# Scales loaded first, first features kept as halves, the last projection begun ahead of weight loads, the last norm by tiles: an attention and feed-forward block on one core

## The chip, the core and the metric

The kernel runs on one core of a Trainium2 chip. The core has a matrix engine (TensorE, PE), a vector engine (DVE), a scalar engine (ACT), GpSimd (POOL) and a queue engine (SP) that issues most of the transfers; ACT and POOL issue a few. The working memory is SBUF (128 partitions), matmul results go to PSUM[...], and inputs, outputs and scratch tensors lie in DRAM. The metric is the device time of one execution in microseconds.

## The reference

One token sequence of 4096 tokens with 256 features goes through attention with 16 heads and a feed-forward net, each between two layernorms and with a residual:

```python
x = x + _layernorm(attn(_layernorm(x)))
x = x + _layernorm(ffn(_layernorm(x)))
# attn: causal, 16 heads of 16 features
qkv = x @ w_attn + b_attn
logits = jnp.einsum('bhqd,bhkd->bhqk', q, k) * scale        # causal mask
out = softmax(logits) @ v;  return out @ w_proj + b_proj
# ffn: weights are -1, 0 or 1, each output feature has a scale
_tlin = lambda x, w, s: jnp.einsum('bsi,oi->bso', x, w) * s
h = silu(_tlin(x, w1_w, w1_s)) * _tlin(x, w2_w, w2_s)       # 256 -> 1024
h = gelu(_tlin(h, h1_w, h1_s))                               # 1024 -> 1024
h = gelu(_tlin(h, h2_w, h2_s))
return _tlin(h, w3_w, w3_s)                                  # 1024 -> 256
```

All inputs and the output are float32.

## The kernel before

The tokens are cut into eight blocks of 512 (`QB`, `NB` = 8), each of four tiles of 128 tokens (`NT`). The program has two stages. From `manual_schedule` on, the order of the instructions on every engine is the order in which the Python program issues them; only the few instructions ahead of it are placed by a scheduler.

**Attention.** `prep(j)` normalizes block j of x, transposes it into `xT` (ACT copy, L460), and makes queries, keys and values. The main loop goes over 32 items (j, g): a block of queries and a group of four heads. For each it makes products of queries and keys twice: once for the row maxima (`MaxUnit`, reduced on DVE), and once for the exponentials (`ScoreUnit`, ACT); on the diagonal POOL masks the exponentials (L611). `Values` multiplies them with the values and with a column of ones, so that each head's row sums come out beside the weighted values. The result of an item is copied by ACT to `av_sb` (L650) and stored by SP to a DRAM scratch (`avd`, L652).

**Background work.** `Background` holds a queue of generators. Each `yield True` ends a step; the loop calls `step()` or `pace()` between its own instructions, and a step issues what lies up to the next yield. `prep` runs there, and `project(j)`: it loads x again and the row sums (L187, L191), after three steps takes their reciprocals on DVE (L194), stores these to DRAM (L196), loads the weighted values and, spread over partitions, the reciprocals (L200, L201), multiplies them on POOL (L208), multiplies with the projection's weights (TensorE, L218), takes the layernorm, adds x and stores the block (`x1`, L240). `norm_block(j)` loads such a block, normalizes it and transposes it (L260) to features on partitions; its callback `done` receives the two PSUM banks. During the last items of attention it is run for block 0, with `first_features` as the callback (ACT copies to `xT0`, L718). Projections of blocks 0 to 6 run in attention, that of block 7 in the feed-forward.

**Weights.** `halve_weights` rounds the ternary weights to the float32r type and tests whether they fit it exactly; `flag` says so, and a branch (`values_load`, L1006, L1007) takes `feed_forward(True)` where they do. The profiled run took it.

**Feed-forward.** Every activation is kept as two float32r halves, high and low part, and each product is made once for either. The loop goes over the eight blocks: `w1` and `w2` (eight feature chunks, `za`, `zb`), Silu on ACT, product on DVE (`fa`, L961), `settle` on DVE into the halves `ha` (L910, L911); two layers `h1`, `h2` (eight chunks each, Gelu on ACT, L974, `settle`); and `w3` by tiles of tokens (`pyf`, L987), scaled by `s3` on DVE (L994). After the fourth tile the block's layernorm follows (L996 to L999) and one store (L1000). After every chunk there is one `bg.step()`, in the two layers of block 0 two. At the start, `keep_features(0)` splits `xT0` into halves (ACT L925, DVE L927), SP issues sixteen loads of the `h2` weights (L174) and one of `w3` (L885), and only then, from the first steps, what `project(7)` loads. Four scale vectors and the broadcast `s3` are loaded by POOL's queue between the stages (L837, L846).

Buffers: in attention `o` and `inv` hold a projection's inputs, `T` the transposed block; in the feed-forward `activations(2, ..)` takes tiles of a pool with two buffers.

Of the kernel before, what the change touches and what calls it, by code (L numbers as in the profile page):

```python
# [10 lines left out]
F32 = mybir.dt.float32  # L11
F32R = mybir.dt.float32r
AF = mybir.ActivationFunctionType
ALU = mybir.AluOpType
# [3 lines left out]
P = 128  # L18
QB = 512
# [48 lines left out]
def sandwich_kernel(  # L68
# [70 lines left out]
        nc.vector.bn_aggr(mv[:, t, :], st)  # L139

    def layernorm_rstd(mv):
        ve = stat.tile([P, NT], F32, tag="ve", name="ve")
        nc.vector.tensor_scalar_add(ve, mv[:, :, 1], EPS)  # L143
        rstd = stat.tile([P, NT], F32, tag="rstd", name="rstd")
        nc.gpsimd.tensor_tensor(rstd, ve, neghalf, ALU.pow)  # L145
        return rstd

    def normalize(dst, src, mv, rstd, t, engine=nc.vector):
        engine.tensor_scalar(  # L149
            dst, src, mv[:, t, 0:1], rstd[:, t : t + 1], ALU.subtract, ALU.mult  # L150
        )
# [119 lines left out]
        mybir.EngineType.SP,  # L271
    }


    xT0 = const.tile([P, DC, QB], F32, tag="xT0", name="xT0")


    with ExitStack() as actx:
# [16 lines left out]
        class Room:  # L295
# [3 lines left out]
                return two_banks(name)[:, 0, :]  # L299

            def features(self, j):
                return [wk1.tile([P, DC, QB], F32, tag=t, name=f"{t}_{j}") for t in ("o", "inv")]

            def tokens(self, j):
                return wk1.tile([P, NT, D], F32, tag="y", name=f"y_{j}")
# [409 lines left out]

        def first_features(pts):
            for c in range(DC):
                nc.scalar.copy(xT0[:, c, :], pts[c])  # L718

        items = [(j, g) for j in range(NB) for g in range(G)]  # L720
        count = [NT * (j + 1) for j, g in items]
# [110 lines left out]
        bg.finish()  # L832


    def load_scale(pool, src, tag):
        s = pool.tile([P, FC], F32, tag=tag, name=tag)
        nc.gpsimd.dma_start(out=s, in_=src.rearrange("(c p) -> p c", p=P))  # L837
        return s

    fs = ctx.enter_context(tc.tile_pool(name="fs", bufs=1))  # L840
    s1 = load_scale(fs, w1_s, "s1")
    s2 = load_scale(fs, w2_s, "s2")
    sh1 = load_scale(fs, h1_s, "sh1")
    sh2 = load_scale(fs, h2_s, "sh2")
    s3 = fs.tile([P, D], F32, tag="s3", name="s3")
    nc.gpsimd.dma_start(out=s3, in_=w3_s.partition_broadcast(P))  # L846

    def feed_forward(halves):


# [4 lines left out]
        with ExitStack() as fctx:  # L855
# [23 lines left out]

            w3_r = fw.tile([P, FC, D], F32R, tag="w3", name=f"w3_{parts}")  # L880
            w3_sb = w3_r.bitcast(F32)
            if halves:
                tiles = {**W, "h2": weight_pieces("h2", TAGS["h2"])}
                load_pieces(rounded["h2"], tiles["h2"])
# [14 lines left out]
            def activations(n, name):  # L899

                return [
                    hp.tile([P, n, QB], F32, tag=f"h{n}{p}", name=f"{name}{p}")
                    for p in "hl"[:parts]
                ]

# [15 lines left out]
            def keep_features(j):  # L921
                def done(pts):
                    xT = xTs[j] = activations(DC, f"xTf{parts}_{j}")
                    for c in range(DC):
                        nc.scalar.copy(single(xT[0][:, c, :]), pts[c])  # L925
                        if halves:
                            nc.vector.tensor_tensor(  # L927
                                single(xT[1][:, c, :]),
                                pts[c],
                                single(xT[0][:, c, :]),  # L930
                                ALU.subtract,
                            )
                return done
# [12 lines left out]
                        )  # L946
                return ps

            room, bg = Room(), Background()
            keep_features(0)([xT0[:, c, :] for c in range(DC)])  # L950
            bg.add("project", project(NB - 1, room), PROJECT)
            for j in range(NB):
                xT = xTs[j]
                ha = activations(FC, f"ha{parts}_{j}")
                for oc in range(FC):
                    za = linear("w1", oc, xT, DC, f"za{parts}_{j}_{oc}")
                    zb = linear("w2", oc, xT, DC, f"zb{parts}_{j}_{oc}")
                    sl = f2.tile([P, QB], F32, tag="sl", name=f"sl{parts}_{j}_{oc}")
                    nc.scalar.activation(sl, za, AF.Silu, scale=s1[:, oc : oc + 1])  # L959
                    h = chunk(ha, oc, f"fa{parts}_{j}_{oc}")  # L960
                    nc.vector.scalar_tensor_tensor(  # L961
                        h, zb, s2[:, oc : oc + 1], sl, ALU.mult, ALU.mult
                    )
                    settle(ha, oc, h)
                    bg.step()
                if j + 1 < NB:
                    bg.add("norm", norm_block(j + 1, room, keep_features(j + 1)), NORM)
                src = ha
                for layer, (key, sc) in enumerate((("h1", sh1), ("h2", sh2))):
                    hb = activations(FC, f"hb{parts}_{j}_{layer}")  # L970
                    for oc in range(FC):
                        z = linear(key, oc, src, FC, f"z{parts}_{j}_{layer}_{oc}")
                        h = chunk(hb, oc, f"fb{parts}_{j}_{layer}_{oc}")
                        nc.scalar.activation(h, z, AF.Gelu, scale=sc[:, oc : oc + 1])  # L974
                        settle(hb, oc, h)
                        bg.step()
                        if j == 0:
                            bg.step()
                    src = hb
                bg.finish()  # L980
                y = f1.tile([P, NT, D], F32, tag="yf", name=f"yf{parts}_{j}")
                mv = stat.tile([P, NT, 2], F32, tag="mv", name=f"mvo{parts}_{j}")
                for t in range(NT):
                    ps = ps_f.tile([P, QB], F32, tag="f", name=f"pyf{parts}_{j}_{t}")
                    for c in range(FC):
                        for i, part in enumerate(src):
                            nc.tensor.matmul(  # L987
                                ps[:, 0:D],
                                lhsT=single(part[:, c, t * P : (t + 1) * P]),
                                rhs=(w3_r if halves else w3_sb)[:, c, :],  # L990
                                start=(c == 0 and i == 0),
                                stop=(c == FC - 1 and i == parts - 1),
                            )
                    nc.vector.tensor_tensor(y[:, t, :], ps[:, 0:D], s3, ALU.mult)  # L994
                    layernorm_stats(y[:, t, :], mv, t)
                rstd = layernorm_rstd(mv)  # L996
                for t in range(NT):
                    normalize(y[:, t, :], y[:, t, :], mv, rstd, t)
                    nc.gpsimd.tensor_tensor(y[:, t, :], y[:, t, :], xb[j][:, t, :], ALU.add)  # L999
                nc.sync.dma_start(  # L1000
                    out=out[j * QB : (j + 1) * QB, :].rearrange("(t p) d -> p t d", p=P),
                    in_=y,
                )


    low = nc.values_load(flag, min_val=0, max_val=1)  # L1006
# [38 lines left out]
```

## Time and profile before

| | us |
|---|---|
| median of 3 runs | 2574.32 (2571.3 to 2575.26) |
| the profiled execution | 2574.63 |
| its span, first to last instruction | 2572.9 |
| TensorE busy | 2439.2 |
| DVE busy | 1824.1 |
| ACT busy | 1257.2 |
| POOL busy | 575.2 |
| first score matmul (L508) | 61.73 |
| last attention product (L641) starts | 1852.89 |
| first feed-forward matmul (L940) starts | 1857.38 |
| last store issued (L1000) | 2567.23 |

Times in the trace's answers count from the first instruction. In a timeline each row is a start, a duration, the engine (PE is a matmul, PEld the load of its weights, SPq the issue of a transfer), the source line, the operation, and `out<-in` with the shapes; in brackets stands how long the engine was idle before it and what released it. The page cuts the span into 40 slices of 64.3 us and gives the busy share of each in tenths.

### The profile page before, as it was taken

The numbers are of one execution on the slowest core, as the hardware profiler recorded it, in microseconds if no ns is written. First come the engines' busy times: TensorE is split into PE (matmuls) and PEld (weight loads), VectorE is DVE, ScalarE is ACT, GpSimd is POOL, SyncE is SP. The second block draws the span as 40 slices with busy tenths as digits, with TensorE's granted clock in tenths as the row PEclk, the third lists the DMA queues.
The fourth block names the chain that finished last, engine by engine and source line by source line (L and its number), as shares of the span: only waits on it lengthen the run. The fifth ranks groups of instructions, "written<-read, shape, count | busy, mean of one in ns | idle before, by whom it ended". The sixth has DMA issues, their size and how long they took to land. (4 is left out here: it accounts for less than half of the span.)

```text
span 2572.9 us, 40118 instructions
## 1 busy us (share of the span) xinstructions
PE 2439.2 (95%) x15237; PEld 1444.8 (56%) x15237; DVE 1824.1 (71%) x3965; ACT 1257.2 (49%) x1490; POOL 575.2 (22%) x869
## 2 busy tenths in 40 slices
PE   5899999999999999999999999999989999999998
PEld 2454445445445544554455554544468877887786
DVE  2687788879788987898899898986055445544553
ACT  1335466556566655666577666766712222222221
POOL 2325333332242234322322222000120000000000
PEclk8779899899999999999999999999999999999999
DMA  4444244232233323324212232111120000000000
GB/s 156 144 152 154 88 135 153 99 129 74 91 108 123 120 83 130 109 79 141 66 62 95 83 96 72 57 45 55 42 90 17 17 1 17 17 17 1 17 9 10
DMA packets 134777, 202.73 MB, mean 79 GB/s; under 512 B 14864, under 2 KB 59536, under 8 KB 134576
## 3 DMA queue, kind: packets, MB, share of 16 engines
q1 hardware_dynamic: 132624, 198.75, 23.3%
q8 instruction: 122, 2.00, 0.3%
q10 hardware_dynamic: 1776, 1.18, 0.2%
q0 software_dynamic: 176, 0.15, 0.1%
q14 instruction: 79, 0.65, 0.1%
HBM read 137.91 MB, written 62.13 MB: 78 GB/s over the span
## 5 line engine op out<-in xcount | busy, mean ns | idle before, releaser
L606 ACT ACTIVATE e<-s 128x1024 f32<-128x1024 f32 (+3 forms) x1175 | 1040.6, 936 | 618.5 <-PE s L591 611.5
L521 DVE TENSOR_REDUCE mx<-pm 128x1 f32<-128x512 f32 x1792 | 1112.4, 682 | 160.4 <-PE pm L508 145.8
L508 PE MATMUL pm<-k,q 64*128 64x512 f32 (+3 forms) x2304 | 636.8, 460 | 56.8 <-DVE mx L521 40.7
L508 PEld LDWEIGHTS pm<-k,q 64*128 64x128 f32 x2304 | 326.5, 190 | 567.3 <-DVE mx L521 394.7
L641 PE MATMUL av<-e,v 128*32 128x512 f32 (+3 forms) x4608 | 591.1, 584 | 2.9 <-POOL e L611 2.9
L591 PE MATMUL s<-q,k 64*128 64x512 f32 (+3 forms) x2304 | 476.3, 395 | 7.6 <-DVE y L226 3.1
L591 PE MATMUL s<-mrow,ones 64*128 64x512 f32 (+3 forms) x2304 | 461.6, 384 | 0.0
L525 DVE CUSTOM_DVE_ANT_0 pm<-pm,mask 128x384 f32<-128x384 f32 (+3 forms) x512 | 239.8, 517 | 75.3 <-PE pm L508 71.4
L974 ACT ACTIVATE fb<-z,sh 128x512 f32<-128x512 f32 x128 | 88.1, 688 | 396.6 <-PE z L940 377.8
L591 PEld LDWEIGHTS s<-q,k 64*128 64x128 f32 x2304 | 237.0, 191 | 79.0 <-issue 19.3
L591 PEld LDWEIGHTS s<-mrow,ones 64*128 64x128 f32 x2304 | 241.8, 191 | 38.6 <-DVE mrow L565 0.7
L611 POOL TENSOR_SCALAR_AFFINE_SELECT e<-e 128x256 f32<-128x256 f32 x256 | 102.2, 407 | 647.6 <-ACT e L606 645.9
L145 POOL TENSOR_TENSOR rstd<-ve,neghalf 128x4 f32<-128x4 f32 x32 | 32.9, 1027 | 847.7 <-DVE ve L143 822.1
L940 PE MATMUL z<-hb_0h,h 128*128 128x512 f32 x512 | 203.7, 398 | 0.0
L940 PE MATMUL z<-hb_0l,h 128*128 128x512 f32 x512 | 202.2, 395 | 0.0
L641 PEld LDWEIGHTS av<-e,v 128*32 128x32 f32 x4608 | 92.6, 109 | 148.8 <-issue 130.0
L910 DVE CAST hb_1h<-fb 128x512 fp32r<-128x512 f32 x64 | 27.4, 428 | 149.9 <-ACT fb L974 149.9
L910 DVE CAST hb_0h<-fb 128x512 fp32r<-128x512 f32 x64 | 27.5, 430 | 139.4 <-ACT fb L974 139.4
L940 PEld LDWEIGHTS z<-hb_0h,h 128*128 128x128 f32 x512 | 96.8, 189 | 22.9
L940 PEld LDWEIGHTS z<-hb_0l,h 128*128 128x128 f32 x512 | 96.8, 189 | 22.1
L959 ACT ACTIVATE sl<-za,s 128x512 f32<-128x512 f32 x64 | 44.1, 689 | 131.4 <-DVE fa L961 66.4
L693 POOL CAST wh<-wc 128x256 fp32r<-128x256 f32 x88 | 34.9, 397 | 261.8 <-DMA wc<-in_h_t_dram 197.1
(235 smaller groups left out, 2430.9 us busy)
## 6 DMA issues: line engine op xcount, KB each, us to landing
k<-k SPq DMA_DIRECT2D x288, 256.0 KB
q<-q SPq DMA_DIRECT2D x64, 256.0 KB
x<-in_x_dram SPq DMA_DIRECT2D x16, 512.0 KB
k<-hik SPq DMA_DIRECT2D x32, 256.0 KB
k<-lok SPq DMA_DIRECT2D x32, 256.0 KB
q<-hiq SPq DMA_DIRECT2D x32, 256.0 KB
q<-loq SPq DMA_DIRECT2D x32, 256.0 KB
avd<-av_sb SPq DMA_DIRECT2D x32, 256.0 KB
```

The source lines that it names most:

```text
L508: nc.tensor.matmul(ps[:, 0:n], lhsT=qT[j, g][pr][r, t * P : (t + 1) * P], rhs=kT[G * j + g, c, pr][r, 0:n], start=True, stop=True,)
L521: nc.vector.tensor_reduce(self.mx[:, h, c : c + 1], ps[:, 0:n], AX.X, ALU.max)
L525: nc.vector.tensor_tensor_reduce(out=ps[:, 0:n], in0=ps[:, 0:n], in1=mask[:, QB - n : QB], scale=1.0, scalar=-3.0e38, op0=ALU.add, op1=ALU ...
L591: nc.tensor.matmul(self.ps[i][:, self.q0 :], lhsT=(self.k, ones[pr])[m][r, :], rhs=(qT[j, g][pr], mT[j, g])[m][r, self.q0 :], start=(m == ...
L606: nc.scalar.activation(e[:, at : at + n, q0:], ps[:, :, q0:], AF.Exp)
L611: nc.gpsimd.affine_select(out=at, in_=at, compare_op=ALU.is_ge, fill=0.0, base=0, pattern=[[0, 2], [1, P]], channel_multiplier=-1,)
L641: nc.tensor.matmul(self.av[h * HW : (h + 1) * HW, q0:], lhsT=vb[kt // NT][:, kt % NT, o : o + HW], rhs=es[h // 2][:, h % 2, q0:], start=(k ...
L693: nc.gpsimd.tensor_copy(hi, w)
L910: nc.vector.tensor_copy(hi, full)
L940: nc.tensor.matmul(ps, lhsT=w[c], rhs=single(part[:, c, :]), start=(c == 0 and i == 0), stop=(c == kc - 1 and i == parts - 1),)
L959: nc.scalar.activation(sl, za, AF.Silu, scale=s1[:, oc : oc + 1])
L974: nc.scalar.activation(h, z, AF.Gelu, scale=sc[:, oc : oc + 1])
```

## The change

Five things are edited. (1) The four scales and `s3` are loaded at the program's start, still on POOL's queue, into the pool of constants. (2) `first_features` writes block 0's features as two halves during attention: ACT copies the high part, DVE subtracts it from the PSUM bank for the low part. The feed-forward uses them directly, so that `keep_features(0)` goes. To make room, the projection in attention shares the buffer `T` with `prep` in place of a buffer `inv`, and the feature tiles of the feed-forward move to a pool with one buffer. (3) `project(7)` is created and advanced to its first yield ahead of the loads of `h2` and `w3`, so its loads of x and of the row sums come before them in SP's queue; the later steps of the projection each come one step earlier. (4) The layernorm at the end of a block is a function `leave`; for the last block it runs for every tile of tokens one tile behind, with an rstd and a store for each. (5) The last addition of the last tile is on DVE, the others stay on POOL.

```diff
--- before.py
+++ after.py
@@ -139,10 +139,11 @@
         nc.vector.bn_aggr(mv[:, t, :], st)
 
     def layernorm_rstd(mv):
-        ve = stat.tile([P, NT], F32, tag="ve", name="ve")
+        n = mv.shape[1]
+        ve = stat.tile([P, n], F32, tag=f"ve{n}", name="ve")
         nc.vector.tensor_scalar_add(ve, mv[:, :, 1], EPS)
-        rstd = stat.tile([P, NT], F32, tag="rstd", name="rstd")
-        nc.gpsimd.tensor_tensor(rstd, ve, neghalf, ALU.pow)
+        rstd = stat.tile([P, n], F32, tag=f"rstd{n}", name="rstd")
+        nc.gpsimd.tensor_tensor(rstd, ve, neghalf[:, 0:n], ALU.pow)
         return rstd
 
     def normalize(dst, src, mv, rstd, t, engine=nc.vector):
@@ -271,8 +272,22 @@
         mybir.EngineType.SP,
     }
 
-
-    xT0 = const.tile([P, DC, QB], F32, tag="xT0", name="xT0")
+    def load_scale(pool, src, tag):
+        s = pool.tile([P, FC], F32, tag=tag, name=tag)
+        nc.gpsimd.dma_start(out=s, in_=src.rearrange("(c p) -> p c", p=P))
+        return s
+
+    s1 = load_scale(const, w1_s, "s1")
+    s2 = load_scale(const, w2_s, "s2")
+    sh1 = load_scale(const, h1_s, "sh1")
+    sh2 = load_scale(const, h2_s, "sh2")
+    s3 = const.tile([P, D], F32, tag="s3", name="s3")
+    nc.gpsimd.dma_start(out=s3, in_=w3_s.partition_broadcast(P))
+
+
+    xT0 = [
+        const.tile([P, DC, QB], F32R, tag=f"xT0{p}", name=f"xT0{p}") for p in "hl"
+    ]
 
 
     with ExitStack() as actx:
@@ -299,7 +314,7 @@
                 return two_banks(name)[:, 0, :]
 
             def features(self, j):
-                return [wk1.tile([P, DC, QB], F32, tag=t, name=f"{t}_{j}") for t in ("o", "inv")]
+                return [wk1.tile([P, DC, QB], F32, tag=t, name=f"{t}o_{j}") for t in ("o", "T")]
 
             def tokens(self, j):
                 return wk1.tile([P, NT, D], F32, tag="y", name=f"y_{j}")
@@ -715,7 +730,9 @@
 
         def first_features(pts):
             for c in range(DC):
-                nc.scalar.copy(xT0[:, c, :], pts[c])
+                hi, lo = (t[:, c, :] for t in xT0)
+                nc.scalar.copy(hi, pts[c])
+                nc.vector.tensor_tensor(lo, pts[c], hi, ALU.subtract)
 
         items = [(j, g) for j in range(NB) for g in range(G)]
         count = [NT * (j + 1) for j, g in items]
@@ -832,19 +849,6 @@
         bg.finish()
 
 
-    def load_scale(pool, src, tag):
-        s = pool.tile([P, FC], F32, tag=tag, name=tag)
-        nc.gpsimd.dma_start(out=s, in_=src.rearrange("(c p) -> p c", p=P))
-        return s
-
-    fs = ctx.enter_context(tc.tile_pool(name="fs", bufs=1))
-    s1 = load_scale(fs, w1_s, "s1")
-    s2 = load_scale(fs, w2_s, "s2")
-    sh1 = load_scale(fs, h1_s, "sh1")
-    sh2 = load_scale(fs, h2_s, "sh2")
-    s3 = fs.tile([P, D], F32, tag="s3", name="s3")
-    nc.gpsimd.dma_start(out=s3, in_=w3_s.partition_broadcast(P))
-
     def feed_forward(halves):
 
 
@@ -879,6 +883,9 @@
 
             w3_r = fw.tile([P, FC, D], F32R, tag="w3", name=f"w3_{parts}")
             w3_sb = w3_r.bitcast(F32)
+            room, bg = Room(), Background()
+            last_projection = project(NB - 1, room)
+            next(last_projection)
             if halves:
                 tiles = {**W, "h2": weight_pieces("h2", TAGS["h2"])}
                 load_pieces(rounded["h2"], tiles["h2"])
@@ -899,7 +906,9 @@
             def activations(n, name):
 
                 return [
-                    hp.tile([P, n, QB], F32, tag=f"h{n}{p}", name=f"{name}{p}")
+                    (f1 if halves and n == DC else hp).tile(
+                        [P, n, QB], F32, tag=f"h{n}{p}", name=f"{name}{p}"
+                    )
                     for p in "hl"[:parts]
                 ]
 
@@ -946,9 +955,30 @@
                         )
                 return ps
 
-            room, bg = Room(), Background()
-            keep_features(0)([xT0[:, c, :] for c in range(DC)])
-            bg.add("project", project(NB - 1, room), PROJECT)
+            xTs[0] = [t.bitcast(F32) for t in xT0]
+            if not halves:
+                xTs[0] = activations(DC, "xTf0")
+                nc.vector.tensor_tensor(xTs[0][0], *xT0, ALU.add)
+            bg.add("project", last_projection, PROJECT)
+            due = []
+
+            def leave(j, y, mv, ts, rstd):
+
+                for i, t in enumerate(range(ts.start, ts.stop)):
+                    nc.vector.tensor_scalar(
+                        y[:, t, :], y[:, t, :], mv[:, t, 0:1], rstd[:, i : i + 1],
+                        ALU.subtract, ALU.mult,
+                    )
+                    (nc.vector if (j, t) == (NB - 1, NT - 1) else nc.gpsimd).tensor_tensor(
+                        y[:, t, :], y[:, t, :], xb[j][:, t, :], ALU.add
+                    )
+                nc.sync.dma_start(
+                    out=out[j * QB + ts.start * P : j * QB + ts.stop * P, :].rearrange(
+                        "(t p) d -> p t d", p=P
+                    ),
+                    in_=y[:, ts, :],
+                )
+
             for j in range(NB):
                 xT = xTs[j]
                 ha = activations(FC, f"ha{parts}_{j}")
@@ -993,14 +1023,14 @@
                             )
                     nc.vector.tensor_tensor(y[:, t, :], ps[:, 0:D], s3, ALU.mult)
                     layernorm_stats(y[:, t, :], mv, t)
-                rstd = layernorm_rstd(mv)
-                for t in range(NT):
-                    normalize(y[:, t, :], y[:, t, :], mv, rstd, t)
-                    nc.gpsimd.tensor_tensor(y[:, t, :], y[:, t, :], xb[j][:, t, :], ALU.add)
-                nc.sync.dma_start(
-                    out=out[j * QB : (j + 1) * QB, :].rearrange("(t p) d -> p t d", p=P),
-                    in_=y,
-                )
+                    if j == NB - 1:
+
+                        one = slice(t, t + 1)
+                        due.append((j, y, mv, one, layernorm_rstd(mv[:, one, :])))
+                        while len(due) > (t < NT - 1):
+                            leave(*due.pop(0))
+                if j < NB - 1:
+                    leave(j, y, mv, slice(0, NT), layernorm_rstd(mv))
 
 
     low = nc.values_load(flag, min_val=0, max_val=1)
```

## The prediction

> **What bounds the kernel now.** First the page: TensorE is busy in 95% of the span, so an edit counts only where TensorE stands still or a serial stretch lies open. The slices tell where: full from the third slice on except around slice 29, at the change of stage.
>
> ```profile
> PE 2439.2 (95%) x15237; PEld 1444.8 (56%) x15237; DVE 1824.1 (71%) x3965; ACT 1257.2 (49%) x1490; POOL 575.2 (22%) x869
> PE   5899999999999999999999999999989999999998
> PEclk8779899899999999999999999999999999999999
> ```
>
> Then the timeline of single engines where the diff works. At the change of stage, POOL's and TensorE's rows (start, duration, then in brackets the idle time and its releaser):
>
> ```profile
> 1850.65 0.41 POOL L611 TENSOR_SCALAR_AFFINE_SELECT e<-e 128x256 f32<-128x256 f32 x1 [0.39 <-ACT e L606]
> 1851.26 1.14 POOL L837 DMA_DIRECT2D s<-in_w_s_dram  x1 [0.20 <-issue]
> 1852.42 0.42 POOL L611 TENSOR_SCALAR_AFFINE_SELECT e<-e 128x256 f32<-128x256 f32 x1
> ...
> 1852.89 0.41 PE L641 MATMUL av<-e,v 128*32 128x128 f32 x4 [1.36 <-POOL e L611]
> 1857.38 0.80 PE L940 MATMUL za<-xTf_0h,w 128*128 128x512 f32 x1 [4.08 <-ACT xTf_0h L925]
> ```
>
> A scale's load sits in POOL's queue between the last two masks, so TensorE waits 1.36 us; then 4.08 us for the copy of the first features (L925), whose target is free only when the last attention store has landed. Further on, DVE, TensorE and the end:
>
> ```profile
> 1876.94 0.55 DVE L194 RECIPROCAL sums<-sums 128x64 f32<-128x64 f32 x1 [7.63 <-DMA sums<-avd]
> 1878.12 0.51 PE L940 MATMUL z<-ha_0h,h 128*128 128x512 f32 x1 [3.42 <-DVE fa L961]
> 1926.01 2.21 PE L260 MATMUL ptf<-ident,yn 128*128 128x128 f32 x8 [3.75 <-DVE yn L149]
> 2562.70 1.02 POOL L145 TENSOR_TENSOR rstd<-ve,neghalf 128x4 f32<-128x4 f32 x1 [79.86 <-DVE ve L143]
> 2563.75 2.19 DVE L149 TENSOR_SCALAR yf<-yf,mvo,rstd 128x256 f32<-128x256 f32 x4 [1.13 <-POOL rstd L145]
> 2564.24 2.96 POOL L999 TENSOR_TENSOR yf<-yf,x 128x256 f32<-128x256 f32 x4 [0.53 <-DVE yf L149]
> 2567.23 0.38 SPq L1000 DMA_DIRECT2D out_dram<-yf  x1
> ```
>
> DVE stands 7.63 us before block 7's reciprocal because its input was asked for at 1869.12, behind 5 MB of weights. The last block's norm is one serial chain after the last matmul. The start is serial too, and DVE and TensorE wait there for loads:
>
> ```profile
> 9.09 0.17 DVE L320 TENSOR_SCALAR bqk<-bqk 128x2 f32<-128x2 f32 x1 [9.09 <-DMA bqk<-in_b_attn_dram]
> 9.49 2.04 PE L756 MATMUL pb<-wp,bv 128*128 128x256 f32 x4 [9.49 <-DMA wp<-in_w_proj_dram]
> ```
>
> [...] the mean clock is 0.51 in 1855-1862 and 0.79 in 1878-1886 and in 1926-1934 (3.4 us of 8 at half), each beside a stall of 3.4 to 4.1 us, with matmuls 0.43 us apart instead of 0.23. So a stall that goes takes some 1.5 us more with it, and a new one of that length brings it back. [...] the sums, issued last on SP's queue, landed last; and while the scale loads ran (1857 to 1861) the core moved 312, 210, 130 and 145 GB/s against some 365 after.
>
> **The change part by part.** The sum is against the profiled execution (2574.63 us, span 2572.9), 0.3 us above the median of 2574.32.
>
> *Scales first, at the start: a loss.* The five POOL loads now begin at about 1 us; they issue in 1.14+0.91+1.75+0.57 = 4.4 us. POOL has that: after its memsets it waits from 3.5 to 14.4, and ident, now 1.1 us later, is first read at 9.17. But the DMA engines have not: their share is 0.94, 1.08 and 1.17 in the three windows from 2 to 8 us, and bqk and wp land at the end of that. Bounds: the loads' own 0.14 MB at 380 GB/s is 0.4 us; from the rates above, four microseconds at 200 instead of 365 lose 1.9 us in the worst stretch, and with the earlier scale loads some 3.5. Everything up to the first scores hangs on this chain, so I take +2.0, range +0.3 to +3.5.
>
> *Halves of the first features.* In attention, two subtractions from PSUM are added on DVE (L927's kind, 0.69 us each). They also hold both score buffers longer: TensorE's next scores waited for the second copy until 1719.67, and would wait for the second subtraction until about 1720.5. +0.8; from 0 (DVE has 2.3 us free soon after) to +1.7.
>
> *The change of stage.* With POOL's queue clear, the last mask starts at 1851.1 and the last products at 1851.55 instead of 1852.89: -1.34. Nothing is copied, so the first feed-forward matmul has only the branch (0.5 us of flag load) before it: about 1852.4 instead of 1857.38. What is late next is ACT: in the new order the Silu table load (1.28) itself waits for za, so Silu ends at 1853.5+1.28+0.69 and the first fa runs at 1855.55 instead of 1861.57. From there DVE sets the pace, 1.86 us for each of eight features, as in later blocks. 6.0 us earlier.
>
> *Projection begun ahead.* The load of x and of the sums are the first things SP issues after the last attention store; the sums wait for that store to land (2.7 us after its issue in the trace, so 1855.4), and the sixteen h2 loads behind them start at 1856, 1.4 us later than now. They are not needed until the second layer, 50 us on. The reciprocal stands one feature earlier and finds its sums there: the 7.63 us go. First-layer product 0 ended at about 1885.2; now it ends at 1855.55+15.3+0.5+0.35 = 1871.7: 13.5 us earlier.
>
> Then comes a new wait. The reciprocals' store and the two row-sum loads come after h2 and w3 in SP's order. 5 MB at 362 KB/us from 1857 are through at 1871.1, so the store lands at about 1872.3. In the trace POOL's first product began 5.16 us after the store's landing, its second 7.48; without one 256 KB load, which now goes ahead (1.4 us at 180 KB/us), that is 1876.0 and 1878.4, and the second ends at 1879.7. The new order puts half of the projection after product 1 (3.72 us), at 1875.4, where formerly both halves came after product 2. TensorE therefore stands 4.4 us, and with the half clock loses 1.7 more. Product 3 starts at 1879.75+1.8+3.7+1.8+1.7 = 1888.8 instead of 1895.88. So of the 13.5 us stay 7.1. If the inverse came in time 13.2 would stay; if it came 4 us later still, 3.5.
>
> *The shifted steps.* As every step is one earlier, the variance of block 7's tokens is issued right after product 3's start, not behind its settling, and block 1's normalization stands before the settling of second-layer feature 1. Relative to product 3 it started at 29.57 us (1925.45); now: product 0 of the second layer ends at 22.3, Gelu 0.7, settling 1.1, statistics 0.8, rstd 1.2, hence 26.15. The transposes wait some 0.6 us instead of 3.75[...]: -3.4 and -1.2. Block 1's load comes at 17.4 after product 3's start, before DVE has settled feature 6 at 16.8 plus its own work, so it adds at most 0.6 on DVE, whose result is needed later. -4.6, range -2 to -5.
>
> *The last norm by tiles.* Only tile 3 remains after the last matmul: up to ve unchanged (2562.6), rstd 1.0, normalize 0.4, add on DVE 0.45, with POOL's add of tile 2 (0.8) beside it; the two stores go one after the other at 2564.55 and 2565.0, against 2567.23. The last store is 128 KB instead of 512, which took 1.7 us in packets: -1.2. More small instructions on DVE and POOL beside the matmuls (POOL 1.0+0.8 of 1.92 us for a tile) may delay tile 3 by 0.3. -3.2, range -2 to -4.5.
>
> *At nothing.* The inverse shares the buffer of xT: projections and preparations follow each other in one queue, and the nearest pair in the trace (last use of xT at 130, load of the inverse at 166.6) has 36 us between. Single feature buffers in the feed-forward: the first layer has read them before the next norm writes. If either cover were gone it would show as new idle time of ACT before L460 or before the xTf copies.
>
> Sum: +2.0+0.8-7.1-4.6-3.2 = -12.1. From the median: 2562.2 us.
>
> **Rivals.** (1) The inverse comes in time, because the weights drain faster than 362 KB/us now that no scale loads are between: -18.3, 2556. For it: 370-390 in undisturbed microseconds; against: that is 1 us, and 4.4 are missing. (2) The inverse is 3 us later than I say or the start loses its full price: -7 to -9, 2566. For it: SP's issues took up to 1.49 us each with a deep queue. (3) Slower: the shifted start changes the clock of the first 330 us. The slices show it at 0.7 to 0.9 there, and a half-clock window of 3.4 us costs 1.7. It decides only from ten additional windows (17 us against 12.1): about 2580. [...] (4) The gains vanish: the first feed-forward matmul still waits, since its bank or ACT's table holds it, and the new wait eats the rest: 2572.
>
> **How the numbers follow.** Main case 0.50; (1) 0.20; (2) 0.17; (3) 0.07; (4) 0.06. The predicted time is the main case's, 2562.2. Bounds of its parts reach from -18 to -5; the range 2555.5 to 2570 leaves out cases (3), (4) and the edges of (1) and (2). A measurement of this kernel tells about 0.2%, 5.1 us, from no change, so faster means below 2569.2: the main case, (1), and most of (2), 0.83; same 0.10; slower 0.07.
>
> **What would show it.** Right: bqk and wp landing at 11 to 12 us; the first scores' stage shifted by as much; no wait of the last products on a mask over 0.3 us; first L949 matmul (za) under 1 us after the last product; no wait of DVE before the reciprocal; a wait of py for POOL of 3 to 6 us followed by half clock; transposes of block 1 waiting under 1 us; the last store 4 us after the last matmul. Wrong: a za that waits 3 us or more, a py without a wait, or a first score at an unchanged time.

## The result, and the profile after

| | before | changed |
|---|---|---|
| median, us | 2575.3 (2571.3 to 2576.84, 6 runs) | 2557.97 (2555.09 to 2564.41, 6 runs) |
| ratio to before | | 0.9939, 95% interval 0.9924 to 0.9953 |
| profiled execution, us | 2574.63 | 2558.75 |
| its span, us | 2572.9 | 2557.0 |

The change makes the kernel 0.6% faster, 17 us where 12 were forecast. First the page of the changed kernel: the busy time of the engines, the slices of TensorE and its clock.

```profile
PE 2424.5 (95%) x15237; PEld 1442.7 (56%) x15237; DVE 1822.2 (71%) x3969; ACT 1256.1 (49%) x1488; POOL 575.1 (22%) x871
...
PE   4899999999999999999999999999989999999998
...
PEclk8789999899999999999999999999999999999999
```

TensorE's busy time fell by 14.7 us (2439.2 to 2424.5) with the same 15237 matmuls. Idle time that goes does not lower busy time, so something else must have happened too: the matmuls themselves take less time. The slices do not show it, because it is spread thin.

The timeline at the start, then at the change of stage:

```profile
11.92 0.17 DVE L335 TENSOR_SCALAR bqk<-bqk 128x2 f32<-128x2 f32 x1 [11.92 <-DMA bqk<-in_b_attn_dram]
12.61 2.05 PE L773 MATMUL pb<-wp,bv 128*128 128x256 f32 x4 [12.61 <-DMA wp<-in_w_proj_dram]
...
1852.64 0.77 PE L656 MATMUL av<-e,v 128*32 128x128 f32 x8 [0.17 <-POOL e L626]
1853.46 0.58 ACT L665 COPY av_sb<-av 128x512 f32<-128x512 f32 x1 [1.13 <-PE av L656]
1854.10 0.50 PE L949 MATMUL za<-xT0h,w 128*128 128x512 f32 x1 [0.69 <-ACT av_sb L665]
1855.37 1.28 ACT L989 ACT_TABLE_LOAD   x1 [1.32 <-PE za L949]
1857.38 0.75 DVE L991 SCALAR_TENSOR_TENSOR fa<-zb,s,sl 128x512 f32<-128x512 f32 x1 [71.92 <-ACT sl L989]
1863.19 0.55 DVE L195 RECIPROCAL sums<-sums 128x64 f32<-128x64 f32 x1
1883.01 1.22 PE L219 MATMUL py<-wp,oi_2h 128*128 128x256 f32 x2 [5.90 <-POOL oi_2h L209]
1886.53 2.93 PE L219 MATMUL py<-wp,oi_2h 128*128 128x256 f32 x6 [2.30 <-POOL oi_2h L209]
1921.74 1.64 PE L261 MATMUL ptf<-ident,yn 128*128 128x128 f32 x8 [0.88 <-DVE yn L150]
```

wp lands 3.1 us later than before (12.61, not 9.49). The wait for the last mask is 0.17 us instead of 1.36, that of the first feed-forward matmul 0.69 instead of 4.08, and the reciprocal has no bracket: it no longer waits. The projection's matmuls (py) have a new wait of 5.90 + 2.30 us. Block 1's transposes (ptf) wait 0.88 instead of 3.75. At the end of the program (the rows are the last tile's, except the four stores, of which the first is for tile 0):

```profile
2548.01 4.75 SPq L975 DMA_DIRECT2D out_dram<-yf  x4
...
2550.52 0.58 POOL L146 TENSOR_TENSOR rstd<-ve,neghalf 128x1 f32<-128x1 f32 x1 [0.64 <-DVE ve L144]
...
2551.13 0.81 DVE L968 TENSOR_SCALAR yf<-yf,mvo,rstd 128x256 f32<-128x256 f32 x1 [0.44 <-POOL rstd L146]
2551.98 0.43 DVE L972 TENSOR_TENSOR yf<-yf,x 128x256 f32<-128x256 f32 x1
```

To see where the time comes from, take the same instruction in both traces and subtract its starts; the offset's change from one milestone to the next is what that stretch gained or lost. As in the prediction, the first layer is `h1` and the second `h2`, and a product is one feature chunk of 16 matmuls, whose end the Gelu on ACT marks. (The recorded expectations below count `w1`/`w2` as the first layer, so `h1` and `h2` are the second and third there.) Three of the milestones, first in the kernel before:

```profile
1885.39 0.69 ACT L974 ACTIVATE fb<-z,sh 128x512 f32<-128x512 f32 x1 [3.39 <-PE z L940]
...
1900.04 0.69 ACT L974 ACTIVATE fb<-z,sh 128x512 f32<-128x512 f32 x1 [6.48 <-PE z L940]
...
2561.30 0.42 DVE L994 TENSOR_TENSOR yf<-pyf,s 128x256 f32<-128x256 f32 x1 [0.81 <-PE pyf L987]
```

and then in the changed one:

```profile
1873.50 0.69 ACT L1004 ACTIVATE fb<-z,sh 128x512 f32<-128x512 f32 x1 [3.11 <-PE z L949]
...
1899.19 0.69 ACT L1004 ACTIVATE fb<-z,sh 128x512 f32<-128x512 f32 x1 [4.68 <-PE z L949]
...
2549.08 0.42 DVE L1024 TENSOR_TENSOR yf<-pyf,s 128x256 f32<-128x256 f32 x1 [0.30 <-PE pyf L1017]
```

| up to | offset, us | this stretch |
|---|---|---|
| last but one attention item (copy of `av_sb`) | +1.5 | +1.5 |
| Gelu of the first layer's product 0 | -11.9 | -13.4 |
| Gelu of its product 3 | -0.85 | +11.0 |
| last Gelu before block 1's transposes | -1.4 | -0.55 |
| next Gelu, after the transposes | -5.8 | -4.4 |
| last `yf` scaling (L1024) | -12.2 | -6.4 |
| end of span | -15.9 | -3.7 |

The fourth and sixth rows are the surprise: almost nothing of the diff runs there, and yet 7 us come from them, in steps of 0.09 us per product of 16 matmuls.

### The profile page after: what moved, and what is told of

Same layout as the page of the kernel before. It is cut to its first block, busy times and chain, and to the rows that moved or that the text cites. A ratio compares the mean times of both kernels' runs of the same rounds, so it can differ in the third digit from the quotient of the medians.

```text
span 2557.0 us, 40127 instructions
## 1 busy us (share of the span) xinstructions
PE 2424.5 (95%) x15237; PEld 1442.7 (56%) x15237; DVE 1822.2 (71%) x3969; ACT 1256.1 (49%) x1488; POOL 575.1 (22%) x871
## 5 line engine op out<-in xcount | busy, mean ns | idle before, releaser
L146 POOL TENSOR_TENSOR rstd<-ve,neghalf 128x4 f32<-128x4 f32 (+1 forms) x35 | 34.3, 979 | 829.7 <-DVE ve L144 803.7
L991 DVE SCALAR_TENSOR_TENSOR fa<-zb,s,sl 128x512 f32<-128x512 f32 x64 | 47.6, 743 | 71.9 <-ACT sl L989 71.9
```

What stands on the lines that cost most here:

```text
L991: nc.vector.scalar_tensor_tensor(h, zb, s2[:, oc : oc + 1], sl, ALU.mult, ALU.mult)
```

## Experiments

Each is the changed kernel or the kernel before with one thing different. Ratios are to the kernel before, run on the same chip. Single profiled executions of the attention stage differ by several microseconds whatever the edit (its last `av_sb` copy lies between 1846.8 and 1859.0 in fourteen traces), so stretches are read from traces and totals from medians. The changed kernel was not run beside the experiments; where one is compared with it, the difference of the ratios is given too.

**1. The order of the load queue.** h2 and w3 are loaded after the inverse.

```diff
-            if halves:
-                tiles = {**W, "h2": weight_pieces("h2", TAGS["h2"])}
-                load_pieces(rounded["h2"], tiles["h2"])
-            nc.sync.dma_start(
+            tiles = dict(W)
+            def load_rest():
+                if halves:
+                    tiles["h2"] = weight_pieces("h2", TAGS["h2"])
+                    load_pieces(rounded["h2"], tiles["h2"])
+                nc.sync.dma_start(
...
                     settle(ha, oc, h)
                     bg.step()
+                    if (j, oc) == (0, 3):
+                        load_rest()
```

> The changed kernel, but with the loads of h2 and w3 issued after the projection's inverse loads (after the fourth feature) instead of ahead of them. Theory 'order of the load queue': the inverse is late only because its store and loads stand behind 5 MB of weights. Then the reciprocals' store lands near 1866, POOL's two products run before 1873, TensorE's projection matmuls do not wait (8.2 us in the changed kernel) and the half-clock window of 10.2 us beside them goes (5.1 us): some 13 us below the changed kernel, about 2545. Rival 'POOL and DVE, not the queue': the wait of the projection's matmuls shrinks by less than 3 us; about 2555. A further rival: h2 now comes too late for the second layer and the wait moves there; then a wait of TensorE at its first product shows, and the time stays at 2558.

Measured: 2544.36 us (2543.07 to 2552.46), ratio 0.9893 (0.9877 to 0.9909). The timeline of this kernel:

```profile
1854.02 0.57 SPq L192 DMA_DIRECT2D sums<-avd  x1
1860.97 0.34 SPq L197 DMA_DIRECT2D invd<-sums  x1
...
1862.44 0.58 SPq L202 DMA_DIRECT2D oi_2l<-invd  x1
...
1864.56 12.36 SPq L175 DMA_DIRECT2D h<-r_h  x16
...
1866.96 1.29 POOL L209 TENSOR_TENSOR oi_2h<-oi_2h,oi_2l 128x512 f32<-128x512 f32 x1 [16.62 <-DMA oi_2l<-invd]
...
1875.15 1.89 PE L219 MATMUL py<-wp,oi_2h 128*128 128x256 f32 x8
1880.52 1.89 PE L219 MATMUL py<-wp,oi_2h 128*128 128x256 f32 x8
```

POOL's first product begins 6.0 us after the store's issue (1860.97 to 1866.96), where it was 11.7 in the changed kernel (1869.96 to 1881.69), and py has no bracket. From the Gelu of product 0 to that of product 3 this kernel gains 11.3 us on the changed one, and it has kept them at the end of the first layer: nothing comes back as a wait for h2. The order of the queue is the cause of the wait, and this version beats the kernel before by 29 us and the changed kernel by 14 (12 by the ratios).

**2. The scales back between the stages**, their tiles where the change puts them:

```diff
-    s1 = load_scale(const, w1_s, "s1")
...
+    def load_scales():
+        for s, src in ((s1, w1_s), (s2, w2_s), (sh1, h1_s), (sh2, h2_s)):
+            nc.gpsimd.dma_start(out=s, in_=src.rearrange("(c p) -> p c", p=P))
+        nc.gpsimd.dma_start(out=s3, in_=w3_s.partition_broadcast(P))
...
+    load_scales()
     def feed_forward(halves):
```

> The changed kernel, but with the five loads of the scales issued where the kernel before has them, between the stages (their tiles stay where the change puts them). Theory 'the start pays for the scales': wp lands at 9.5 again instead of 12.6, the stage of the attention begins 3 to 5 us earlier, and the last mask waits again (+1.4 us at the change of stage). If the offset of the start lasts, the time is 2 to 4 us below the changed kernel; rival 'the attention stage gives the offset back by itself' (in the trace of the changed kernel +5.2 us at 324 us had become -0.3 at 1694): the offset at 1694 is the same as in the changed kernel within 1 us, and the time 1 to 2 us above it because of the mask.

Measured: 2554.69 us (2550.65 to 2566.53), ratio 0.993 (0.991 to 0.995), which overlaps the changed kernel's interval. In the trace wp lands at 11.2, not at the 9.5 expected (in experiment 11, which has no scale loads at the start either, it lands at 9.75). The attention stage is 2 to 3 us earlier than in the changed kernel from 116 to 900 us and stands at -0.15 at 1694; the mask then costs 1.2. The trace is the rival's picture, the median, 2 to 3 us below the changed kernel's, the theory's: the spread hides a price of that size, and the question stays open.

**3. The last norm by tiles alone**, on the kernel before (the diff's `leave`, `due` and `layernorm_rstd`):

> The kernel before with only the last norm taken tile by tile. Forecast in the prediction -3.2, read in the two traces as -3.7: 2571.6. The pace of the second and third layers' matmuls (232 ns apart in the kernel before, 227 in the changed one) must be that of the kernel before, 232, if the placement of the features' buffers or the order of the loads sets it; 227 here would say that it differs from one execution to the next, or hangs on something that this small edit moves too. Rival: last norm worth less than 1 us, since the second last tile's work delays the last tile's: 2575.

Measured: 2571.51 us (2564.85 to 2575.57), ratio 0.999 (0.9982 to 0.9997), against 2573.69. In the trace the last scaling is 4.3 us later than in the kernel before and the span only 0.9 longer: 3.4 us won at the end (2.2 by the medians, interval 0.8 to 4.6). Its matmuls in `h1` and `h2` stay 232 ns apart.

**4. The first features as halves and the feature buffers alone** (with them the inverse in the buffer of `xT`), on the kernel before:

```diff
-                nc.scalar.copy(xT0[:, c, :], pts[c])
+                hi, lo = (t[:, c, :] for t in xT0)
+                nc.scalar.copy(hi, pts[c])
+                nc.vector.tensor_tensor(lo, pts[c], hi, ALU.subtract)
...
-                    hp.tile([P, n, QB], F32, tag=f"h{n}{p}", name=f"{name}{p}")
+                    (f1 if halves and n == DC else hp).tile(
+                        [P, n, QB], F32, tag=f"h{n}{p}", name=f"{name}{p}"
+                    )
...
-            keep_features(0)([xT0[:, c, :] for c in range(DC)])
+            xTs[0] = [t.bitcast(F32) for t in xT0]
```

> The kernel before with only the first features kept as halves and the feature buffers moved (features of the feed-forward in single buffers, the inverse in the buffer of xT); scale loads, order of the loads and last norm as before. Theory 'placement': the second and third layers' matmuls stand 227 ns apart, which alone gives some 10 us by the end (128 products of 16 matmuls, 0.09 us each, less what is hidden). Rival 'not the placement': 232 ns. The first feed-forward matmul starts without the copy, some 3 to 4 us earlier; the reciprocal still waits for the sums behind the weights (7 us or more), so that most of the earlier start is lost again, and block 1's transposes wait about 3.7 us as before. Time with the pace: about 2562; without it about 2573.

Measured: 2573.06 us (2569.41 to 2579.22), ratio 0.9998 (0.999 to 1.0007). The pace stays at 232. The first `fa` is 3.4 us earlier relative to the last attention copy, and after the reciprocal, still waiting for its sums, nothing of it is left. Without the new load order the halves are worth nothing that these runs show.

**5 and 6. Where the pace comes from.** In experiments 1 and 2 it was 227, in 3 and 4 it was 232: neither scale loads, h2 loads, last norm nor feature pool decides it alone. What goes with it is where the tiles lie in SBUF. Counted from the weights' pieces (2048 bytes per partition each), the activation buffers `ha`, `hb` lie at a remainder to 2048 of 1152 bytes in the kernel before and in 3 and 4, and of 0 in the changed kernel and in 1 and 2. The 1152 bytes are the pool of the scales (four tiles of 32 bytes and 1024 for `s3`), which the kernel before opens ahead of the feed-forward's pools and which edit (1) moves to the constants; experiment 2 puts back the loads, not the tiles. So one empty buffer is put ahead of them, in the kernel before (224 floats or 896 bytes, remainder 0, shown here) and in the changed one (288 floats or 1152 bytes):

```diff
+            if halves:
+                pad = fctx.enter_context(tc.tile_pool(name="pad", bufs=1))
+                pad.tile([P, 224], F32, tag="pad", name="pad")
             hp = fctx.enter_context(tc.tile_pool(name="hp", bufs=2 if halves else 3))
```

> The kernel before with 896 bytes per partition left empty ahead of the feed-forward's activation buffers, and nothing else. In the kernel before those buffers (ha, hb) begin 1152 bytes past a multiple of 2048 as counted from the weights' pieces, in the changed kernel at exactly a multiple; the 896 bytes bring the kernel before to a multiple as well. Theory 'relative address': the second and third layers' matmuls go from 232 to 227 ns apart, the products from 3.72 to 3.63 us, and the time falls by 8 to 11 us, to about 2564. Rival 'the order of the changed kernel's loads and steps sets the pace': 232 ns and an unchanged time, 2574.

> The changed kernel with 1152 bytes per partition left empty ahead of the same buffers, which gives them the distance to the weights' pieces that the kernel before has. Theory 'relative address': the pace falls back to 232 ns and the time rises by 8 to 11 us above the changed kernel, to about 2567. Rival 'order of loads and steps': 227 ns and an unchanged time, 2558. If this kernel turns to 232 and the padded kernel before stays at 232, some other address counts than the distance to the weights.

Measured: the padded kernel before 2564.3 us (2560.1 to 2568.41), ratio 0.9971 (0.9958 to 0.9983); the padded changed kernel 2569.01 (2563.16 to 2580.18), ratio 0.9991 (0.9978 to 1.0003). The groups of instructions of one line (out<-in, shapes, count, busy time in us and mean of one in ns, idle time before) in the window 1960 to 2540, for the kernel before, the kernel before padded, the changed kernel and the changed kernel padded:

```profile
L940 PE MATMUL z<-hb_0h,h 128*128 128x512 f32 x421 | 167.0, 397 | 0.0
```

```profile
L943 PE MATMUL z<-hb_0h,h 128*128 128x512 f32 x448 | 174.9, 390 | 0.0
```

```profile
L949 PE MATMUL z<-hb_0h,h 128*128 128x512 f32 x447 | 174.5, 390 | 0.0
```

```profile
L952 PE MATMUL z<-hb_0h,h 128*128 128x512 f32 x425 | 167.6, 394 | 0.0
```

The counts differ because some records are missing. One matmul lasts longer (390 ns and more) than the gap to the next, so they overlap, and the pace is read from starts. Nine gaps in the timeline of the kernel before take 2.09 us (232 ns each), in the padded one 2.04 (227):

```profile
2099.69 0.39 PE L940 MATMUL z<-hb_0l,h 128*128 128x512 f32 x1
...
2101.78 0.39 PE L940 MATMUL z<-hb_0h,h 128*128 128x512 f32 x1
```

```profile
2099.76 0.39 PE L943 MATMUL z<-hb_0l,h 128*128 128x512 f32 x1
...
2101.80 0.39 PE L943 MATMUL z<-hb_0h,h 128*128 128x512 f32 x1
```

Both turned as the address theory said. From Gelu to Gelu a product takes 3.72 us in the kernel before and 3.63 padded, 3.63 in the changed kernel and 3.73 padded (a mean gap of 233 ns). The time went down by 8 us and up by 11 (13 by the ratios). So a pad of 896 bytes in the kernel before is worth 0.3%, and the changed kernel with the old distance cannot be told from the kernel before.

**7 to 10. Which distances.** The changed kernel with pads of 256, 512, 1024 and 2048 bytes in the same place.

> The changed kernel with 256 bytes per partition left empty ahead of the activation buffers (distance to the weights' pieces 256 past a multiple of 2048). So far every kernel with distance 0 ran the second and third layers' matmuls 227 ns apart, every kernel with 1152 at 230 to 232. Theory 'only a multiple of 2048': slower than 227, and about 2567. Theory 'a multiple of 256 is enough': 227, and about 2558.

> The same with 512 bytes. Theory 'only a multiple of 2048': slower than 227, about 2567. Theory 'a multiple of 512 (one matmul's weights take 512 bytes of a partition) is enough': 227, about 2558.

> The same with 1024 bytes. Theory 'only a multiple of 2048': slower than 227, about 2567. Theory 'a multiple of 1024 or less is enough': 227, about 2558.

> The same with 2048 bytes, the control: if the distance counts by its remainder to 2048, the pace is 227 ns and the time that of the changed kernel, 2558. Rival 'the address itself counts, or padding as such costs': slower than 227 here too.

Measured: 2558.26, 2558.2, 2556.82 and 2558.51 us (ratios 0.994, 0.9944, 0.9935 and 0.9947), all four at 227 ns. "Only a multiple of 2048" falls. What the runs allow is: every kernel at a multiple of 256 ran `h1` and `h2` at 227, every kernel at 1152, which is 128 past a multiple of 256, at 232 to 233. The traces themselves hold a control. In the changed kernel the features of block 0 lie in `xT0` among the constants, by the planner's addresses 32 bytes off a multiple of 256 from the weights, and those of the later blocks at a multiple of 2048. Nine gaps of the same line take 2.09 us (232 ns each) in block 0 and 2.04 (227) in block 1:

```profile
1857.94 0.40 PE L949 MATMUL za<-xT0h,w 128*128 128x512 f32 x1
...
1860.03 0.40 PE L949 MATMUL za<-xT0l,w 128*128 128x512 f32 x1
```

```profile
1957.04 0.39 PE L949 MATMUL za<-xTf_1l,w 128*128 128x512 f32 x1
...
1959.08 0.39 PE L949 MATMUL za<-xTf_1h,w 128*128 128x512 f32 x1
```

In the changed kernel with 1152 bytes of pad, whose later features lie ahead of the pad, these stay at 227 while `h1` and `h2` behind it stand at 233. So it is a matter of the operands' place, not of the whole program. All pads of 256 to 2048 leave a buffer's own address as it was, too, counted modulo 256: whether the distance or that address counts was not told apart, and why either should is open.

**11. The scales in the middle of attention**, with h2 late:

```diff
+            if (j, g) == (2, 0):
+                load_scales()
```

> The changed kernel with h2 and w3 loaded after the projection's inverse, and with the scales' five loads issued at the first item of the third block's attention instead of at the start. Theory 'the start pays': against the kernel with late h2 alone (2544.4) wp lands 3 us earlier and the last mask stays free, so 2541, of which the attention stage's changing clock may take or give 3 us. Rival 'the attention stage gives the start's offset back': 2544, no difference within 1 us. Rival 'the loads cost there too': more than 2545, with POOL's masks or the halving of the weights late beside them.

Measured: 2546.81 us (2544.73 to 2551.31), ratio 0.99 (0.9883 to 0.9918); with late h2 alone 2544.36. wp lands at 9.75, the first attention copy is 3.4 us earlier, and by 328 us the lead is gone; at the end of attention it is 3 us behind. No gain: the same as experiment 1 within its interval.

**12. The steps of the projection where they were**, the loads still first:

```diff
-        for _ in range(3):
+        for _ in range(4 if j == NB - 1 else 3):
             yield True
         nc.vector.reciprocal(sums, sums)
```

> The changed kernel with one empty step put ahead of block 7's reciprocal, so that every background step stands where the kernel before has it, while the loads of x and of the sums stay first in the queue. Theory 'the shift of the steps removed the stall at block 1's transposes': that stall returns to 3 to 4 us (0.9 in the changed kernel) with half clock beside it, +4.4 us; and the projection's matmuls, both after product 2 again, wait some 3 us less than in the changed kernel: in sum 2558 to 2560. Rival 'the stall went for another reason, such as DVE's earlier work': the transposes wait under 1 us here too, and the time falls to about 2555.

Measured: 2558.59 us (2551.78 to 2567.6), ratio 0.9948 (0.993 to 0.9966). Its timeline:

```profile
1876.87 0.70 PE L219 MATMUL py<-wp,oi_2h 128*128 128x256 f32 x2 [0.67 <-POOL oi_2h L209]
1880.89 4.86 PE L219 MATMUL py<-wp,oi_2h 128*128 128x256 f32 x14 [3.32 <-POOL oi_2h L209]
...
1914.92 2.21 PE L261 MATMUL ptf<-ident,yn 128*128 128x128 f32 x8 [3.75 <-DVE yn L150]
```

The transposes' stall is back at exactly its old 3.75 us, and py waits 4.0 us instead of 8.2. Some of that is not the step's: the sums were issued 2.5 us after the store here, 4.3 in the changed kernel, and kernels of the changed order with 2.6 wait 6.0 to 7.4, so the step itself is worth 2 to 3.4. Both halves of the expectation hold, and they nearly cancel: the shift of the steps was worth its 4.4 us, and was paid with an earlier claim on a late inverse.

## Why the prediction was right, and where it was not

The total was in the range, but by luck in part: two errors offset each other, a wait that was priced too low and a gain that was not seen. By its own steps, with the offset of +1.5 us that the attention stage left taken off the times of the trace:

| step | predicted | measured |
|---|---|---|
| start and halves | +2.8 | +1.5 |
| change of stage, up to product 0 | -13.5 | -13.4 |
| of that, left at product 3 | -7.1 | -2.4 |
| shifted steps, block 1's transposes | -4.6 | -4.4 |
| last norm | -3.2 | -3.7 |
| pace of the two layers | not seen | -7.0 |
| sum | -12.1 | -16 |

*Start and halves.* wp was late by 3.1 us, in the range though above the value taken, and the first score matmul by 4.2 (65.91, not 61.73). That this reaches the end was not shown. Mean of the last attention copy: 1853.5 in the eight traces with scales at the start, 1851.8 in the six others (five of which include the mask's delay). Against a spread of 3 to 4 us in either group that is no finding, and the medians of experiments 2 and 11 have opposite signs. The +1.5 of this one trace is inside that spread. The halves alone gave no visible loss.

*The change of stage* went as worked out: first matmul at 1852.6 (1852.4 predicted), first `fa` at 1855.9 (1855.55), no wait of the reciprocal. Two small waits were not in the sum: the first matmul waits 0.69 us for ACT's last `av_sb` copy, and the last mask still holds the products for 0.17.

*The step that failed is the price of the new wait.* "TensorE therefore stands 4.4 us, and with the half clock loses 1.7 more." It stood 8.2 and lost 2.9 more. The mechanism was right: TensorE came there when expected (1875.6, 1875.4 predicted), and experiment 1 shows that the order of the queue makes the wait. The term that was mis-sized is the arrival of the inverse. The queue in the changed kernel:

```profile
1854.07 0.32 SPq L667 DMA_DIRECT2D avd<-av_sb  x1
1854.62 0.38 SPq L113 DMA_DIRECT2D x<-in_x_dram  x1
1858.39 0.57 SPq L192 DMA_DIRECT2D sums<-avd  x1
1859.15 9.79 SPq L175 DMA_DIRECT2D h<-r_h  x16
1869.29 0.37 SPq L892 DMA_DIRECT2D w<-r_w  x1
1869.96 0.33 SPq L197 DMA_DIRECT2D invd<-sums  x1
...
1877.67 0.57 SPq L202 DMA_DIRECT2D oi_2l<-invd  x1
```

The sums could be issued 4.3 us after the store, 2.7 were assumed. The load of the reciprocals, which waits for their store, could be issued at 1877.67, or 1876.2 with the offset taken off, against the 1872.3 predicted: 3.9 us late. In between lie 5 MB, which ran from about 1860 to 1876, some 320 KB/us, where 362 were assumed. The windows of the changed kernel show the slow beginning (last two columns: share of the DMA engines, GB/s):

```profile
1860.00:1862.00 2.00, 2.00 (x10) 1.60 (x9) 1.93 (x4) 0.69 (x1) 0.00 (x0) 1.00 0.78 254
1862.00:1864.00 2.00, 2.00 (x10) 1.59 (x9) 1.93 (x5) 0.69 (x1) 0.00 (x0) 1.00 1.01 261
1864.00:1866.00 2.00, 2.00 (x10) 1.63 (x9) 1.93 (x4) 0.69 (x1) 0.00 (x0) 1.00 0.97 320
1866.00:1868.00 2.00, 2.00 (x11) 1.59 (x10) 1.93 (x4) 0.69 (x1) 0.00 (x0) 1.00 0.99 348
```

The 362 was a rate of the full stream, used from its first byte. The prediction had put the slow stretch of the kernel before down to the scale loads beside it; here the stream begins slowly without them. Kernels with the same order in which the sums were issued 2.6 us after the store still wait 6.0 to 7.4 us (pads of 2048, 1024 and 1152), so the late sums are the smaller part. Two traces show what the place in the queue costs here: from the issue of the reciprocals' store to that of the load that waits for it pass 7.7 us behind the 5 MB (1869.96 to 1877.67), and 1.5 in experiment 1, where the 5 MB come after (1860.97 to 1862.44). The forecast looked at the right place, and should have asked what the order would be worth if turned round: 11 us.

*The shifted steps and the last norm* were sized within 0.5 us of the trace, and experiments 12 and 3 show each by itself. That the transposes' wait would come without half clock was an estimate; beside the 0.88 us of the changed kernel the clock is full (1.00 from 1916 to 1932).

*The pace was not seen.* Under "At nothing" the prediction looked for waits on the two buffers that are shared or made single; of the scales it priced the loads, and not the 1152 bytes that their tiles leave free ahead of `ha` and `hb`. That place is worth 0.09 us per product. In the changed trace it gave about 10 us, of which two stretches of half clock (at 2143 and 2484, some 1.5 us each) took 3 back. By experiments 5 and 6 it is worth 8 to 13 us of the 17. With the old distance the intended edits bring 2 us (experiment 6, interval 6 gained to 1 lost), as what the change of stage won was mostly handed to the projection's wait.

## What to carry to other kernels

When a load is moved to the front of a queue, ask also for the store and reload that hang on it, and put what is needed last (here weights 50 us early) behind all of them (11.3 us in experiment 1). When the busy time of an engine changes with the same instructions, measure the distance between their starts: a pool that was moved can change the pace of matmuls that no line of the diff names (here from 232 to 227 ns), and a padding run in both kernels settles it cheaply. A total that lands in the range proves no step; compare by milestones.

## What the runs showed of the hardware that was not expected

- The spacing of 512-column matmuls went with the place of the moving operand in SBUF: 227 ns at a distance to the weights of a multiple of 256 bytes (ten kernels), 232 to 233 at 1152 (four), and 232 to 235 for block 0's features in the changed kernel, 32 bytes off such a multiple.
- The next transfer that waited for the last attention store was issued either 2.5 to 2.6 us after it (six traces) or 3.8 to 4.5 (four), in kernels with nearly the same instructions there; what decides is open.
- The two stretches of half clock in the changed kernel, at 2143.2 and 2484.6, last 3.4 us each (clock 0.51 and 0.50). They stand beside no long stall: ahead of either TensorE waits four times, 0.2 to 0.6 us each, and is busy 62 and 61% of the last 3.4 us. The same four waits come in blocks 1, 2, 4, 5 and 6, each time with 3.4 us in which TensorE is busy 61 to 63%, and there the clock stays full. So in this trace the same waits cost some 1.5 us more in two blocks and nothing in five; what decides was not shown.
- rstd on POOL took 0.58 us for one column where it took 1.02 for four.
